# A two-layer graph-attention block on one Trainium2 core: centred linear weights, the context in four 64x64 tiles of the array, variance by squares on ScalarE, blocks prepared across passes, the first block in another order

## The chip, the cores and the metric

The kernel runs on one core of one Trainium2 chip. The core has a matrix engine (TensorE, PE in the profile; PEld is its weight load), a vector engine (VectorE, DVE), a scalar engine (ScalarE, ACT), GpSimd (POOL), and SyncE (SP), which here only issues DMAs. Each engine takes its own instructions in order and waits on semaphores for what others produce. The metric is the device time in microseconds (us) of one execution; the figure for a kernel is the median of its runs.

## The reference

The input `x` is 128 graphs of 64 nodes with 768 features, `adj` a 64x64 mask for each graph. All is fp32. First `h = max(layernorm(x), 0)`. Then two layers, each with three 768x768 weights:

```
u_left  = h @ (h @ W_left.T).T / sqrt(768)         # per graph, 64x64
u_right = h @ (h @ W_right.T).T / sqrt(768)
u       = u_left where j >= i, u_right where j < i, both masked by adj
e       = exp(u) * adj
att     = e / (sum(e, axis=2) + 1e-10)
ctx     = att @ (h @ W_lin.T + b_lin)
h       = max((ctx - mean(ctx)) / (std(ctx, ddof=1) + 0.001) * a + b, 0)
```

The result is `x + h`.

## The kernel before, in words

8192 tokens are cut into 16 *blocks* `u` of 512 tokens, and a block into four quarters `q` of 128 tokens (two graphs). A layer `l` is two *passes* over all blocks; what passes between them goes through DRAM (`H0`, `H1`: the activations, transposed; `ATT`: the attention, as a 128x128 block-diagonal tile for each quarter).

**Pass one** computes the scores. In layer 0 it also normalises `x` (`prepare`: `bn_stats` and `bn_aggr` at L156-157, square root L207, `norm` L194, `turn` with TensorE transposes L200 and ScalarE evictions L201). `project(u, k, g)` computes a third (`g`) of the left (`k=0`) or right (`k=1`) projection. A product of 2x2 blocks is done with seven block products instead of eight (Strassen-Winograd): the table `ORDER` has seven *groups* X, Y, Z, V, X, Z, V, each three matmuls into the PSUM bank of that name (L229), and each is evicted by DVE or ACT (L240 to L250). The seven need sums of the weights (`S1` to `S4`, `sums_w`, L96 to L100) and of the token blocks (`T1` to `T4`, tile `ts`, `sums_t`, L120 to L123, on POOL). `scores(u)` multiplies the block's tokens with the projections, 48 matmuls with 64 output columns each (L263; the two graphs of a quarter go to PSUM partitions 0-63 and 64-127), then mask, exp and division on DVE and ACT, four transposes (L293), and a store of the attention.

**Pass two** computes `h_lin` and the context. A block has two *rounds* `r`, one for each call of `linear(u, r)`: seven groups of three matmuls of 384 columns (L447), evicted by DVE (L452 to L468) with one helper addition on POOL (`u2b`, L457). After the first group of a round stands `finish` of the round before: `context` (L366) multiplies the 128x128 attention of a quarter with its `h_lin`, in two halves of 384 columns, for two quarters, four matmuls; then mean and variance by `bn_stats` on DVE (L156, L157, L380), square root on ACT (L383), reciprocal and bias on DVE (L385 to L388), and `z = ctx * rs + nb` on ACT (L391). In layer 0, `z` is transposed (L413) and evicted with scale, bias and relu (L416). In layer 1, POOL multiplies by `a` (L394) and adds `b` (L395), and DVE does relu and residual into `xr` (L397), which SP stores.

**What sets the order.** The program is written in the order in which each engine is to take its work; nothing reorders it. Small steps are put as functions in one deque (`queue`), and `pump(n)` between the groups emits the next `n`; `flush` emits all. In pass one, `pump(1)` follows each group; in pass two, `pump(3)`. At a pass's start `load(0)` and `prepare(0)` come ahead of the first group, and the sums for the next layer's weights are one step of that queue (`weights`), emitted between groups of blocks 1 and 2 of pass two. PSUM has eight banks: four for X, Y, Z, V (`ps_st`) and four for all else (`ps_aux`).

## Time and profile before

| | |
|---|---|
| three runs | 3298.9, 3294.8, 3292.9 us; median 3294.8 |
| the profiled execution | 3297.7 us, of which the span of the trace is 3295.9 |
| busy | PE 3095.9 us (94%), DVE 1269.5 (39%), POOL 867.5 (26%), ACT 557.6 (17%) |
| granted PE clock | 0.985 of full on average |
| pass one of layer 0 | first matmul group at 43.1 us; last scores end at 1050.8 |
| pass two of layer 0 | first context at 1084.1, last but one at 1649.6 |
| pass one of layer 1 | first group at 1686.4; last scores end at 2660.9 |
| pass two of layer 1 | first context at 2697.4, last but one at 3262.0 |

Reading notes. Each fp32 matmul of the program stands in the trace as two records (a group of three is "x6"). A busy share of PE says that something was in the array, not that it ran at its peak. In brackets behind a row stands how long its engine was idle just before and what ended that.

### The profile page before, as it was taken

Reading aid. Unit: us, or ns where it says so; the run is one execution under the profiler, and the core shown is the slowest. Engines: PE = TensorE matmul, PEld = TensorE weight load, DVE = VectorE, ACT = ScalarE, POOL = GpSimd, SP = SyncE. Lnnn points to the kernel's source line nnn. Section 1 sums busy time; section 2 is a strip of 40 time slices with the busy share of each in tenths; the row PEclk is TensorE's granted clock in tenths of the full one; section 3 lists DMA queues with packets and bytes.
Section 4 is the critical chain, followed back from the end, with each engine's and each line's share of the span. In section 5 each row is a group of like instructions: output and inputs, shape, how many; then the busy total and the mean of one; then the engine's idle time right before and its main releaser. Section 6 shows DMA issues by size and latency. Waiting matters only on the chain.

```text
span 3295.9 us, 37473 instructions
## 1 busy us (share of the span) xinstructions
PE 3095.9 (94%) x15232; PEld 2396.5 (73%) x15232; DVE 1269.5 (39%) x2906; ACT 557.6 (17%) x1169; POOL 867.5 (26%) x541
## 2 busy tenths in 40 slices
PE   5999999999998889999979999999999979898897
PEld 4888888888887555555568888888888855455454
DVE  4333334334332334444422222222222236666665
ACT  1112112111210223233311000000000001111111
POOL 3111111211210332232222211211111036667665
PEclk9999999999999999999989999999999989999999
DMA  4111211211201132322211101101001023343333
GB/s 167 67 52 46 84 48 49 83 46 52 73 37 56 70 112 86 122 83 83 102 64 55 52 26 36 42 26 49 29 26 52 4 91 122 129 150 126 134 128 108
DMA packets 77484, 244.64 MB, mean 74 GB/s; under 512 B 7936, under 2 KB 34048, under 8 KB 67072
## 3 DMA queue, kind: packets, MB, share of 16 engines
q1 hardware_dynamic: 77312, 242.25, 20.2%
q8 instruction: 120, 1.97, 0.2%
q14 instruction: 52, 0.43, 0.0%
HBM read 158.34 MB, written 83.89 MB: 73 GB/s over the span
## 4 chain that ended last, share of the span: by engine, by line
PE 81%; POOL 9%; DVE 5%; DMA 2%; ACT 1%; issue 1%; SPq 1%; POOLq 0%; ACTq 0%; DVEq 0%
PE Z L229 15%; PE V L229 15%; PE X L229 15%; PE Y L229 8%; PE X L447 6%; PE aux L263 5%; PE aux L366 5%; POOL z L395 4%; PE Y L447 4%; PE V L447 4%; POOL z L394 3%; PE Z L447 2%; DVE xr L397 2%; PE aux L413 1%; PE aux L200 1%; DVE u L455 1%
## 5 line engine op out<-in xcount | busy, mean ns | idle before, releaser
L120 POOL TENSOR_TENSOR ts<-ht 128x768 f32<-128x768 f32 x64 | 116.3, 1816 | 1505.5 <-ACT ht L201 742.9
L447 PE MATMUL X<-w_n_A,ht 128*128 128x384 f32 x768 | 282.2, 505 | 61.0 <-DVE n L464 36.4
L229 PE MATMUL X<-ht,w_l_A 128*128 128x256 f32 x1152 | 281.4, 380 | 12.8 <-DMA ht<-h 12.8
L447 PE MATMUL V<-w_n_A,ts 128*128 128x384 f32 x768 | 271.5, 490 | 22.7 <-DVE n L462 22.7
L229 PE MATMUL X<-ht,w_r_A 128*128 128x256 f32 x1152 | 280.0, 379 | 0.0
L229 PE MATMUL V<-ts,w_r_A 128*128 128x256 f32 x1152 | 280.0, 379 | 0.0
L229 PE MATMUL V<-ts,w_l_A 128*128 128x256 f32 x1152 | 280.0, 379 | 0.0
L250 DVE TENSOR_TENSOR n<-V,u 128x256 f32<-128x256 f32 x384 | 162.2, 422 | 284.5 <-PE V L229 283.5
L447 PEld LDWEIGHTS X<-w_n_A,ht 128*128 128x128 f32 x768 | 145.2, 196 | 169.2 <-DVE n L464 54.9
L243 DVE TENSOR_TENSOR u<-Y,s 128x256 f32<-128x256 f32 x192 | 81.5, 424 | 456.0 <-PE Y L229 452.9
L229 PEld LDWEIGHTS X<-ht,w_l_A 128*128 128x128 f32 x1152 | 219.4, 191 | 42.9 <-DMA ht<-h 13.1
L229 PEld LDWEIGHTS V<-ts,w_r_A 128*128 128x128 f32 x1152 | 217.8, 190 | 29.0
L229 PEld LDWEIGHTS X<-ht,w_r_A 128*128 128x128 f32 x1152 | 217.7, 190 | 29.0
L229 PEld LDWEIGHTS V<-ts,w_l_A 128*128 128x128 f32 x1152 | 217.7, 190 | 29.0
L447 PEld LDWEIGHTS V<-w_n_A,ts 128*128 128x128 f32 x768 | 141.1, 190 | 126.9 <-DVE n L462 20.9
L250 DVE TENSOR_TENSOR n<-Z,u 128x256 f32<-128x256 f32 x192 | 80.7, 421 | 359.1 <-PE Z L229 359.1
L457 POOL TENSOR_TENSOR u2b<-u,b 128x384 f32<-128x384 f32 x64 | 63.9, 998 | 574.9 <-DVE rs L385 574.9
L248 ACT COPY n<-X 128x256 f32<-128x256 f32 x192 | 71.5, 372 | 772.2 <-PE X L229 772.2
L397 DVE SCALAR_TENSOR_TENSOR xr<-z,xr 128x768 f32<-128x768 f32 x64 | 135.8, 2123 | 130.2 <-POOL z L395 130.2
L366 PE MATMUL aux<-n,at 128*128 128x384 f32 x512 | 176.1, 486 | 0.7 <-DVE n L464 0.5
L240 ACT COPY s<-X 128x256 f32<-128x256 f32 x192 | 71.6, 373 | 618.1 <-PE X L229 618.1
L263 PE MATMUL aux<-n,ht 128*64 128x128 f32 x3072 | 174.7, 274 | 0.0
(98 smaller groups left out, 4604.1 us busy)
## 6 DMA issues: line engine op xcount, KB each, us to landing
ht<-h SPq DMA_DIRECT2D x48, 1536.0 KB, 7.2
x<-in_x_dram SPq DMA_DIRECT2D x64, 384.0 KB, 7.2
h<-ht SPq DMA_DIRECT2D x16, 1536.0 KB, 6.2
h<-n SPq DMA_DIRECT2D x16, 1536.0 KB, 6.1
xr<-in_x_dram SPq DMA_DIRECT2D x64, 384.0 KB, 3.7
out_dram<-xr SPq DMA_DIRECT2D x64, 384.0 KB, 2.4
adj<-in_adj_dram SPq DMA_DIRECT2D x32, 256.0 KB, 3.5
att<-at SPq DMA_DIRECT2D x32, 256.0 KB, 2.0
```

The lines of the kernel that those rows point to most:

```text
L120: queue.append(lambda: nc.gpsimd.tensor_sub(b["T1"], b["B12"], b["B11"]))
L229: nc.tensor.matmul(p, w[a][:, c, g * P:(g + 1) * P], b[t][:, c, :], start=(new and c == 0), stop=(c == CH - 1), skip_group_check=True)
L240: nc.scalar.copy(s1, p)
L243: nc.vector.tensor_add(u2, p, s1)
L248: nc.scalar.copy(to, pb)
L250: nc.vector.tensor_add(to, pb, (u4 if i == 3 else u2).rearrange("p (b s) -> p b s", s=S))
L263: nc.tensor.matmul(p[h * S:(h + 1) * S, q, :], ht[:, c, b * S:(b + 1) * S], m[c // CH][:, c % CH, b].rearrange("p k j -> p (k j)"), start= ...
L366: nc.tensor.matmul(p[:, :HH], AT[u][:, q, :], hl[:, q, n * HH:(n + 1) * HH], start=True, stop=True)
L394: nc.gpsimd.tensor_mul(z, z, rows["a"])
L395: nc.gpsimd.tensor_add(z, z, rows["b"])
L397: nc.vector.scalar_tensor_tensor(xr, z, 0.0, xr, op0=ALU.max, op1=ALU.add)
L447: nc.tensor.matmul(p, b[t][:, c, r * P:(r + 1) * P], w[a][:, c, :], start=(new and c == 0), stop=(c == CH - 1), skip_group_check=True)
```

## The change

It has five parts.

1. *Centred weights.* `centre` subtracts from each row of `W_lin` its mean over the 768 outputs, and from `b_lin` its mean, so that `ctx` has mean zero. The steps are four DVE reductions of 128x1152 elements and four POOL subtractions for each layer, in the queue of pass one, block 1. Layer 0's `W_lin` is now loaded there too and not at the start.
2. *Variance by squares.* With mean zero, the variance is a sum of squares: one ACT instruction for a quarter (`AF.Square` with `accum_out`), one square root for both quarters, one add and one reciprocal on DVE. `bn_stats`, `bn_aggr`, the scaling of the variance and the bias `nb` are gone from pass two. In layer 1, DVE multiplies by `rs` and `a` in one instruction out of PSUM (`scaled`), POOL only adds `b`.
3. *Context in 64x64 tiles.* The attention is block-diagonal, so its two 64x64 blocks are multiplied apart: eight matmuls with 64 rows and 64 columns of weights, in four places of the array, into four different halves of two two-bank PSUM tiles. For quarters 2 and 3 the two graphs change places; layer 1 loads its adjacency in that order (three DMAs in place of one) and swaps back.
4. *Blocks prepared across passes.* The last block of a pass loads the next pass's first block and makes its token sums; the last transposes of a pass one stand in the next pass (`flush(keep=1)`); in pass two the token sums and the weight sums are single steps, one behind each group (`beside`).
5. *The first block.* The loads of `W_right` follow the first block, the normalisation goes quarter by quarter, and DVE makes the first sums.

`ps_aux` now has two tiles of two banks in place of four of one. The diff, with unchanged lines and repeated patterns left out:

```diff
-    ps_aux = ctx.enter_context(tc.tile_pool(name="ps_aux", bufs=4, space=bass.MemoryType.PSUM))
+    ps_aux = ctx.enter_context(tc.tile_pool(name="ps_aux", bufs=2, space=bass.MemoryType.PSUM))
...
-    def flush():
-        pump(len(queue))
+    def flush(keep=0):
+        pump(len(queue) - keep)
...
+    def centre(l):
+
+        t = W[l, "n"]
+        for a, b in (("A11", "A21"), ("A12", "A22")):
+            m = stat.tile([P, 2, CH], F32, name="wm", bufs=2)
+
+            def means(a=a, b=b, m=m):
+                nc.vector.reduce_sum(m[:, 0], t[a], axis=mybir.AxisListType.X)
+                nc.vector.reduce_sum(m[:, 1], t[b], axis=mybir.AxisListType.X)
+                nc.vector.tensor_add(m[:, 0], m[:, 0], m[:, 1])
+                nc.vector.tensor_scalar_mul(m[:, 0], m[:, 0], 1.0 / H)
+
+            queue.append(means)
+            for s in (a, b):
+                queue.append(lambda s=s, m=m: nc.gpsimd.tensor_sub(
+                    t[s], t[s], m[:, 0].unsqueeze(2).to_broadcast([P, CH, HH])))
...
         t = W[l, kind]
-        eng.tensor_add(t["S1"], t["A21"], t["A22"])
-        eng.tensor_sub(t["S2"], t["S1"], t["A11"])
...
-            def prepare(u):
+            def prepare(u, eng=nc.gpsimd):
...
-                    def turn(c):
-                        p = ps_aux.tile([P, T], F32, name="aux")
-                        for q in range(Q):
...
+                        nc.scalar.activation(ht[:, c0:c0 + 2, :], p, AF.Relu)
...
-                    for c in range(C):
+                        if u == 0:
+                            queue.append(lambda q=q: scale(q, q + 1))
+                            queue.append(lambda q=q: norm(q))
+                    if u:
+                        queue.append(lambda: scale(0, Q))
+                        for q in range(Q):
+                            queue.append(lambda q=q: norm(q))
+                    for c in range(0, C, 2):
                         queue.append(lambda c=c: turn(c))
                     queue.append(lambda: nc.sync.dma_start(H0[u], ht))
-                sums_t(key)
+                if key not in TS:
+                    sums_t(key, eng)
                 queue.append(lambda: masks(u))
...
-                p = ps_aux.tile([P, Q, 2 * S], F32, name="aux")
+                p = ps_aux.tile([P, 2, T], F32, name="aux")[:, 0].rearrange("p (q m) -> p q m", q=Q)
...
-                    if first:
-                        first()
-                    prepare(0)
+                    if l == 0:
+                        load_w(0, "l")
+                        prepare(0, nc.vector)
+
+                        flush(keep=5)
+                        tokens = [queue.popleft() for _ in range(5)]
+                        sums_w(0, "l", nc.vector)
+                        sums = [queue.popleft() for _ in range(4)]
+                        queue.extend(sums[:2] + tokens[:2] + [sums[2], tokens[2], sums[3], tokens[3], tokens[4]])
+                        load_w(0, "r")
+                        sums_w(0, "r", nc.gpsimd)
+                    else:
+                        prepare(0)
                     flush()
...
+                        else:
+                            load_h(2, l, 0)
+                            sums_t((2, l, 0))
                         if u in aside:
                             aside[u]()
...
-            flush()
+            flush(keep=1)
...
+            bm = stat.tile([P, 2], F32, name="bm", bufs=1)
+            nc.vector.reduce_sum(bm[:, 0:1], rows["b1"], axis=mybir.AxisListType.X)
+            nc.vector.reduce_sum(bm[:, 1:2], rows["b2"], axis=mybir.AxisListType.X)
+            nc.vector.tensor_add(bm[:, 0:1], bm[:, 0:1], bm[:, 1:2])
+            nc.vector.tensor_scalar_mul(bm[:, 0:1], bm[:, 0:1], -1.0 / H)
             nc.gpsimd.tensor_sub(rows["b2"], rows["b2"], rows["b1"])
+            nc.vector.tensor_scalar_add(rows["b1"], rows["b1"], bm[:, 0:1])
...
+            def context(u, r):
+
+
+                hl, at = HL[u], AT[u]
+                lo, hi = slice(0, S), slice(S, P)
+                cx = [ps_aux.tile([P, 2, T], F32, name="aux") for _ in range(2)]
                 for n in range(2):
-                    p = ps_aux.tile([P, T], F32, name="aux")
-                    nc.tensor.matmul(p[:, :HH], AT[u][:, q, :], hl[:, q, n * HH:(n + 1) * HH],
-                                     start=True, stop=True)
-                    cx.append(p[:, :HH])
-                z = sp.tile([P, H], F32, name="z", bufs=2 if last else 4)
-                Z[u, q] = z
+                    for (j, k, i) in ((lo, 0, lo), (hi, 0, hi), (lo, 1, hi), (hi, 1, lo)):
+                        q = r + 2 * k
+                        m = n if j == lo else 1 - n
+                        nc.tensor.matmul(cx[k][i, m, :HH], at[j, q, j], hl[j, q, m * HH:(m + 1) * HH],
+                                         start=True, stop=True)
+                return [c[:, :, :HH] for c in cx]
...
-                    xr = sp.tile([P, H], F32, name="xr", bufs=2)
-                    nc.sync.dma_start(xr, x_t[u][q])
-
-                def chain():
-                    mv = stat.tile([P, 2], F32, name="mv1")
-                    mean_var(mv, cx)
-
-                    var = stat.tile([P, 1], F32, name="var")
...
+                for k in range(2):
+                    nc.scalar.activation(zs[k].rearrange(two, n=2), cx[k], AF.Square, accum_out=ss[:, k:k + 1])
+
+                nc.scalar.activation(sd, ss, AF.Sqrt, bias=floor, scale=1.0 / (H - 1.0))
+                nc.vector.tensor_scalar_add(rs, sd, EPS_LN)
+                nc.vector.reciprocal(rs, rs)
+                if last:
+                    def scaled(k):
+                        nc.vector.scalar_tensor_tensor(
+                            zs[k].rearrange(two, n=2), cx[k], rs[:, k:k + 1],
+                            rows["a"].rearrange(two, n=2), op0=ALU.mult, op1=ALU.mult)
+                        nc.gpsimd.tensor_add(zs[k], zs[k], rows["b"])
+
+                    def done(k):
+                        nc.vector.scalar_tensor_tensor(xs[k], zs[k], 0.0, xs[k], op0=ALU.max, op1=ALU.add)
+                        nc.sync.dma_start(out_t[u][r + 2 * k], xs[k])
+
+                    queue.append(lambda: scaled(0))
+                    queue.append(lambda: scaled(1))
+                    queue.append(lambda: None)
+                    queue.append(lambda: done(0))
+                    queue.append(lambda: done(1))
...
+                def scaled():
+                    for k in range(2):
+                        nc.scalar.activation(zs[k].rearrange(two, n=2), cx[k], AF.Copy, scale=rs[:, k:k + 1])
...
+                queue.append(scaled)
+                queue.append(lambda: None)
                 for c0 in range(0, C, 2):
-                    queue.append(lambda c0=c0: part(c0))
+                    queue.append(lambda c0=c0: turn(c0))
                 if r == 1:
                     queue.append(lambda: nc.sync.dma_start(H1[u], OUT[u]))
 
...
-                    pump(3)
-
+                    elif i:
+                        pump(1)
+                    if aside:
+                        aside.popleft()()
+
+            load(0)
...
-                    linear(u, r, before)
+                    beside = deque()
                     if r == 0:
                         if u + 1 < NB:
                             load(u + 1)
+                        elif not last:
+                            load_h(1, 1, 0)
                         if u in aside:
-                            aside[u]()
-                    elif u + 1 < NB:
-                        prepare(u + 1)
-                        flush()
+                            loaded = aside[u]()
+                    else:
+                        kept = list(queue)
+                        queue.clear()
+                        if u + 1 < NB:
+                            sums_t((2, l, u + 1))
+                        elif not last:
+                            sums_t((1, 1, 0))
+                        if u in aside:
+                            loaded()
+                        beside.extend(queue)
+                        queue.clear()
+                        queue.extend(kept)
+                    linear(u, r, before, beside)
+                    while beside:
+                        beside.popleft()()
             finish(NB - 1, 1)
...
+    def one_aside(l):
+        def begin():
+            load_w(l, "n")
+            centre(l)
+            sums_w(l, "n", nc.gpsimd)
+        return begin
+
+    def two_aside(kind):
+        def begin():
+            load_w(1, kind)
+            return lambda: sums_w(1, kind, nc.gpsimd)
+        return begin
+
+    pass_one(0, {1: one_aside(0)})
+    pass_two(0, {1: two_aside("l"), 2: two_aside("r")})
+    pass_one(1, {1: one_aside(1)})
```

Three places show how the instructions now stand. In TensorE's stream, the border from pass one to pass two of layer 0, up to the third group of the new pass (`aux<-n,ht` are the scores of the last block, `aux<-ident,bd` the transposes of its attention). Before:

```order
L229 MATMUL Z<-ht,w_r_S_192 128x256 x3
L229 MATMUL V<-ts,w_r_A_188 128x256 x3
L263 MATMUL aux<-n,ht 64x128 x48
L293 MATMUL aux<-ident,bd_156 128x128 x4
L447 MATMUL X<-w_n_A_201,ht 128x384 x3
L447 MATMUL Y<-w_n_S_206,ts 128x384 x3
```

Now:

```order
L259 MATMUL V<-ts,w_r_A_250 128x256 x3
L293 MATMUL aux<-n,ht 64x128 x48
L497 MATMUL X<-w_n_A_674,ht 128x384 x3
L497 MATMUL Y<-w_n_S_679,ts 128x384 x3
L323 MATMUL aux<-ident,bd_158 128x128 x4
L497 MATMUL Z<-w_n_S_678,ts 128x384 x3
```

The transposes, which wait for the whole chain of DVE and ACT behind the scores, moved behind two groups of the next pass.

In TensorE's stream, one round of pass two, layer 0 (`aux<-n,at` is the context, `aux<-ident,z` the transposes of `z`). Before:

```order
L447 MATMUL X<-w_n_A_201,ht 128x384 x3
L366 MATMUL aux<-n,at 128x384 x4
L447 MATMUL Y<-w_n_S_206,ts 128x384 x3
L447 MATMUL Z<-w_n_S_205,ts 128x384 x3
L413 MATMUL aux<-ident,z 128x128 x4
L447 MATMUL V<-w_n_A_202,ts 128x384 x3
L413 MATMUL aux<-ident,z 128x128 x8
```

Now:

```order
L497 MATMUL X<-w_n_A_674,ht 128x384 x3
L417 MATMUL aux<-n,at 64x384 x8
L497 MATMUL Y<-w_n_S_679,ts 128x384 x3
L497 MATMUL Z<-w_n_S_678,ts 128x384 x3
L497 MATMUL V<-w_n_A_675,ts 128x384 x3
L470 MATMUL aux<-ident,z 128x128 x4
L497 MATMUL X<-w_n_A_677,ht 128x384 x3
L470 MATMUL aux<-ident,z 128x128 x4
```

The context is eight matmuls of 64 columns, and the transposes moved from behind the third group to behind the fourth, fifth and sixth, four each.

In DVE's stream, one round of pass two, layer 1 (`s`, `u`, `n` are evictions of the linear groups; `xr` is the residual step). Before, from the square root's return on:

```order
L455 TENSOR_TENSOR u_16937<-Y,s_16896 128x384
L385 TENSOR_SCALAR rs_16943<-sd_16941 128x1
L386 RECIPROCAL rs_16943<-rs_16943 128x1
L388 SCALAR_TENSOR_TENSOR nb_16946<-mv_16919,rs_16943 128x1
L460 TENSOR_TENSOR u_16956<-Z,u2b 128x384
L397 SCALAR_TENSOR_TENSOR xr<-z,xr 128x768
L462 TENSOR_TENSOR n<-V,u_16956 128x384
L397 SCALAR_TENSOR_TENSOR xr<-z,xr 128x768
L464 TENSOR_TENSOR n<-X,b_14144 128x384
L466 TENSOR_TENSOR n<-Z,u_16937 128x384
L468 TENSOR_TENSOR n<-V,u2b 128x384
```

Now:

```order
L438 TENSOR_SCALAR rs_15575<-sd_15574 128x2
L439 RECIPROCAL rs_15575<-rs_15575 128x2
L505 TENSOR_TENSOR u_15585<-Y,s_15555 128x384
L442 SCALAR_TENSOR_TENSOR z<-aux,rs_15575,a 128x768
L510 TENSOR_TENSOR u_15595<-Z,u2b 128x384
L442 SCALAR_TENSOR_TENSOR z<-aux,rs_15575,a 128x768
L512 TENSOR_TENSOR n<-V,u_15595 128x384
L514 TENSOR_TENSOR n<-X,b_13481 128x384
L448 SCALAR_TENSOR_TENSOR xr<-z,xr 128x768
L516 TENSOR_TENSOR n<-Z,u_15585 128x384
L448 SCALAR_TENSOR_TENSOR xr<-z,xr 128x768
L518 TENSOR_TENSOR n<-V,u2b 128x384
```

The two residual steps stood around the eviction of the first V group and now stand behind the second X and the second Z; both reads of `cx` for `z` are on DVE.

130 lines of the change are left out of this document (49 added, 81 removed).

## The prediction

> **What bounds the kernel now.** First the page: the shares by engine and the chain that ended last.
>
> ```profile
> PE 3095.9 (94%) x15232; PEld 2396.5 (73%) x15232; DVE 1269.5 (39%) x2906; ACT 557.6 (17%) x1169; POOL 867.5 (26%) x541
> PE   5999999999998889999979999999999979898897
> PE 81%; POOL 9%; DVE 5%; DMA 2%; ACT 1%; issue 1%; SPq 1%; POOLq 0%; ACTq 0%; DVEq 0%
> ```
>
> TensorE is the chain for 81%, and the slices below 9 say where it isn't: the start, pass two of layer 0 (slices 13 to 15), the borders of passes, and pass two of layer 1 (33 to 40). Both passes one are matmul back to back, and the change takes none from them. So I read the chain of waits in order of time, pass two of layer 0 (columns: start, us, what).
>
> ```profile
> 1084.06 2.58 PE aux L366 x8
> 1086.63 1.95 PE Y L447 x6
> ...
> 1093.56 0.87 PE aux L413 x8
> 1094.44 1.94 PE X L447 x6
> ...
> 1102.18 2.58 PE aux L366 x8
> ...
> 1649.59 2.58 PE aux L366 x8
> ```
>
> A round is 18.12 us (1084.06 to 1102.18): seven groups at 1.94, 13.58; the context, 2.58; twelve transposes at 0.87/8 = 0.11, 1.31. That is 17.47; the other 0.65 is TensorE waiting on `z`. From the first context to the last in the loop are 565.5 us, 30 rounds. 30 x 18.12 is 543.6; the other 22 us are two long stalls, which the timeline shows on TensorE and on POOL:
>
> ```profile
> 1129.69 2.62 POOL L96 TENSOR_TENSOR w_l_S<-w_l_A,w_l_A 128x1152 f32<-128x1152 f32 x1 [21.33 <-DMA w_l_A<-in_w_left_dram]
> 1141.72 3.58 PE L447 MATMUL Z<-w_n_S,ht 128*128 128x384 f32 x6 [9.81 <-DVE u L460]
> 1188.67 4.00 PE L447 MATMUL Z<-w_n_S,ht 128*128 128x384 f32 x6 [9.75 <-DVE u L460]
> ```
>
> The weight sums, as one step, stand in POOL's queue and wait for their DMA; behind them waits `u2b`, for it DVE, for that TensorE.
>
> Pass two of layer 1, the timeline of two rounds:
>
> ```profile
> 2902.26 3.90 PE L447 MATMUL X<-w_n_A,ht 128*128 128x384 f32 x6 [2.03 <-DVE n L464]
> ...
> 2920.28 0.96 DVE L397 SCALAR_TENSOR_TENSOR xr<-z,xr 128x768 f32<-128x768 f32 x1 [1.23 <-POOL z L395]
> ...
> 2933.76 1.81 POOL L394 TENSOR_TENSOR z<-z,a 128x768 f32<-128x768 f32 x1
> 2933.83 2.54 DVE L397 SCALAR_TENSOR_TENSOR xr<-z,xr 128x768 f32<-128x768 f32 x1 [2.76 <-POOL z L395]
> 2935.64 2.40 POOL L395 TENSOR_TENSOR z<-z,b 128x768 f32<-128x768 f32 x1
> 2936.30 0.55 DVE L462 TENSOR_TENSOR n<-V,u 128x384 f32<-128x384 f32 x1
> 2936.90 2.20 PE L447 MATMUL V<-w_n_A,ts 128*128 128x384 f32 x6 [0.69 <-DVE n L462]
> ```
>
> DVE takes `xr` ahead of the eviction of V, and waits for POOL's multiply and add. While POOL runs, `xr` takes 2.54 instead of 0.96: it starts 0.07 after POOL's instruction and ends 0.8 after that one's end. So DVE is late, and TensorE with it; after 2.03 us of idleness its group even takes 3.90 instead of 2.10. In the chain:
>
> ```profile
> 2697.40 2.58 PE aux L366 x8
> ...
> 3262.00 2.58 PE aux L366 x8
> ```
>
> 564.6 us for 30 rounds, 18.82 each, of which TensorE needs 13.58 + 2.58 = 16.16.
>
> **The change part by part.** The *context* is the open price: the kernel has no matmul with 64 rows of weights. What it has is `scores`, with two 64-column places. The timeline cut off after 50, 200 and 300 ns, and at the end:
>
> ```profile
> 167.75 0.33 PE L263 MATMUL aux<-n,ht 128*64 128x128 f32 x2
> ...
> 167.75 0.44 PE L263 MATMUL aux<-n,ht 128*64 128x128 f32 x4
> ...
> 167.75 0.55 PE L263 MATMUL aux<-n,ht 128*64 128x128 f32 x6
> ```
>
> Records start in pairs, a pair each 0.11 us, which is what one record of 128 columns alone takes (a transpose, 0.11). So the two places work beside one another, at full rate, from the first pair on; 96 records take 5.39 us in the chain (its rows further down), 48 x 0.109 = 5.23 and 0.16 for the change of array shape. With as much for the way back I put 0.35 us. Four places at full rate: eight matmuls cost as two, 2 x 0.645 (a third of a group) = 1.29, plus 0.35, 1.64 us. Bounds: 1.64 if all four run together; 8 x 0.645 + 0.35 = 5.51 if none does. I take 1.64, since both places of the nearest row lose nothing; this is the largest risk.
>
> The Trainium skill (TensorE: Matmul & The Clock Gate, Part 3, Measured speedup) gives 3.07 for four row tiles, not 4: a context of 5.16/3.07 + 0.35 = 2.03, and 25 us more over 64 of them, an estimate. No row here has row tiles.
>
> *Layer 0, pass two.* A round is 13.58 + 1.31 + 1.64 = 16.53 if nothing else stalls. The transposes now come one to three groups later. Their input: two squares on ACT from 1.65 us after the context's start, 768 elements each; by
>
> ```profile
> L391 ACT ACTIVATE z<-aux,nb,rs 128x384 f32<-128x384 f32 x256 | 157.7, 667 | 69.4 <-DVE nb L388 69.1 <-DVE rs L385 0.3
> L201 ACT ACTIVATE ht<-aux 128x512 f32<-128x512 f32 x96 | 57.1, 597 | 80.4 <-PE aux L200 78.6
> L452 DVE TENSOR_TENSOR s<-X,b 128x384 f32<-128x384 f32 x64 | 35.7, 557 | 126.2 <-PE X L447 126.2
> L120 POOL TENSOR_TENSOR ts<-ht 128x768 f32<-128x768 f32 x64 | 116.3, 1816 | 1505.5 <-ACT ht L201 742.9 <-DMA ht<-h 711.3 <-PE V L229 51.3
> ```
>
> about 1.0 each (597 for 512 elements, in proportion, and some more for the sum); then root and reciprocal, 0.7, and two scalings: 6.4, while the fourth group ends at 7.5. Hidden, with 1 us to spare. The eviction of Y waits on DVE behind the reciprocal until 4.4; it is needed by the third group's eviction at 5.5. The weight sums, single steps half a block after their DMA, no longer hold `u2b`: POOL has 4 x 1.8 + 4 x 2.6 + 1.0 = 18.6 us in such a round, with `u2b` near its front. So 30 x 16.53 = 496 for 565.5: **69.6 less**.
>
> *Layer 1, pass two.* TensorE needs 13.58 + 1.64 = 15.22. DVE: seven evictions 3.9, two `scaled` out of PSUM (two of 557, near 1.0 each), two `xr` 0.96 to 2.54, 0.3 small: 8.1 to 11.3. POOL: two additions 3.6, `u2b` 1.0, in every second round 7.2 of token sums: 11.8 at most. Both fit. What is late next: with token sums, `xr` meets a busy POOL twice; counted through, the last V's eviction ends 15.2 us after the context's start, just as the next context wants it. I give 0.13 on average, 15.35: 30 x 15.35 = 460.5 for 564.6, **104.1 less**. The removed `bn_stats` themselves give nothing; DVE had room.
>
> *Borders and start.* Chain and timeline:
>
> ```profile
> 1045.33 5.42 PE aux L263 x96
> ...
> 1748.09 5.39 PE aux L263 x96
> 1808.51 5.39 PE aux L263 x96
> ...
> 2655.47 5.42 PE aux L263 x96
> ```
>
> ```profile
> 14.45 1.36 DVE L96 TENSOR_TENSOR w_l_S<-w_l_A,w_l_A 128x1152 f32<-128x1152 f32 x1 [12.07 <-DMA w_l_A<-in_w_left_dram]
> ...
> 25.97 1.01 DVE L156 BATCH_NORM_STATS2 st<-x 128x6 f32<-128x384 f32 x2
> ...
> 46.18 1.56 PE L229 MATMUL Y<-ts,w_l_S 128*128 128x256 f32 x6 [1.64 <-POOL ts L121]
> ...
> 1066.45 3.66 PE L447 MATMUL X<-w_n_A,ht 128*128 128x384 f32 x6 [11.09 <-issue]
> ...
> 1686.43 2.93 PE L229 MATMUL X<-ht,w_l_A 128*128 128x256 f32 x6 [12.82 <-DMA ht<-h]
> ...
> 2679.44 4.18 PE L447 MATMUL X<-w_n_A,ht 128*128 128x384 f32 x6 [13.48 <-DMA ht<-h]
> ...
> 3291.74 0.96 DVE L397 SCALAR_TENSOR_TENSOR xr<-z,xr 128x768 f32<-128x768 f32 x1 [1.69 <-POOL z L395]
> ```
>
> First border, scores to first context: 38.7 us. Without a gap 5.4, eight groups 15.5, transposes and shape 0.7: 21.6, so **17.1 less**. The third: 41.9; its bias rows land late, as their place is that of the last mask, and the first eviction waits, 1.6: 23.2, **18.7 less**. The second, from the last context in the loop to the first scores: 98.5. Now 14.6 for the rest of the round, 8.2 for the last context with its wait on ACT and twelve transposes, 3 for slow groups after that idleness (the 2.93 above is 1.29 at full speed), 57 for 44 groups of pass one (a block of 60.42 less scores and four transposes is 42 groups, 1.29 each): 82.8, **15.7 less**. Start: `x` lies ahead of `W_left` in the queue; by bytes, 1.5 of 4.1 MB before 14.45 us, it is there by 5.4. Then four quarters in series on DVE and ACT (1.0 + 0.2 + 0.5 + 0.2 + 0.75 each) with one table load, 12; transposes and evictions 5; one sum on DVE: Y at about 23 instead of 46.2, **23 less** (12 if `W_left`'s sums get in between, 27 at best). End: 33.9 from the last context in the loop; now 13.6 to the last context, 10.6 through squares, `scaled`, addition and two `xr`, 3.2 for the store: 27.4, **6.5 less**.
>
> Centring: 8 POOL and 8 DVE instructions in passes one, hidden by POOL idle there (1505.5 us before L120) and DVE idle. DVE's row for 768 elements of reduction is not there; twice 1.36 a step, under the 5 us that four PSUM banks give; without that cover 10 us in all.
>
> Sum: 69.6 + 104.1 + 17.1 + 18.7 + 15.7 + 23 + 6.5 = 254.7. Against the profiled execution: 3297.7 - 254.7 = 3043.0; it lies 2.9 above the median 3294.8, so **3040**.
>
> **The rivals.** (a) *Two places at a time, not four.* Then a context is 4 x 0.645 + 0.35 = 2.93, 64 x 1.29 = 83 more: 3123. For it: no row shows more than two. A rule of the Trainium skill (TensorE: Matmul & The Clock Gate, Part 3, What overlaps and what doesn't) goes this way: matmuls start and end in program order. As the two records of a matmul share a place, the second would hold back the next place: nine steps of 0.322 + 0.35, 3.25 us, 3143. By that rule the scores would begin with a lone record; the trace has two within the first 50 ns, so it speaks against it. (b) *POOL and DVE take over in layer 1.* If the meeting with token sums costs 2 us in every second round and, as at 2902.26, 1.8 more for the slow group behind it: 15 x 3.8 = 57, 3097. For it the 2.54; against it, that V's eviction is no longer behind the first `xr`. (c) *The context's eight matmuls run one by one*, 5.51: 3.87 x 64 = 248 more, 3288, hardly better than before. (d) The other side: *one by one, and each change of place empties the array*, 0.15 more for each: about 6.6, 64 x 4.96 = 317 more, 3357. From 5.6 us for a context the change is slower than before (254.7/64 + 1.64). Against it, the scores, which change place with each matmul. (e) *The change doesn't do what it says:* first blocks are not ready at the borders, since a DMA waits for a buffer; 51 us back, 3091.
>
> **How the numbers follow.** Forecast 0.64 (its own range 3020 to 3075), (a) 0.18, (b) 0.07, (e) 0.04, (c) 0.04, (d) 0.03. The range 3020 to 3142 holds the first, (b), (e) and most of (a). About 0.2%, 6.6 us, is what a measurement of this kernel tells from no change: slower is (d), 0.03; within it, half of (c) and a little, 0.03; faster, 0.94.
>
> **What would show it.** Right: contexts near 1.6 us in the chain, rounds of 16.5 and 15.3, no idleness of TensorE over 5 us between 25 us and the end, a first Y near 23. Wrong: eight context matmuls over 2.9 us; an idle time before X or the context in layer 1 put down to `n`; idleness at a border put down to a DMA.

## The result, and the profile after

The changed kernel takes 3040.95 us (median; 3040.0 to 3042.56), the one before 3295.96 on the same chip (3292.92 to 3298.92). The ratio is 0.9227, with a 95% interval of 0.9211 to 0.9243: 255 us less, and 3040 us had been predicted. The profiled execution took 3040.96 us, its span is 3039.2, and its granted clock was 0.998 (0.985 before).

The page of the changed kernel, with the rows that answer to those shown of before:

```profile
PE 3001.1 (99%) x15744; PEld 2328.2 (77%) x15744; DVE 1061.3 (35%) x2231; ACT 551.6 (18%) x1124; POOL 765.5 (25%) x486
PE   7999999999999999999999999999999999999998
PE 97%; DVE 1%; DMA 1%; ACT 0%; issue 0%; POOL 0%; DVEq 0%; POOLq 0%; ACTq 0%; SPq 0%
```

TensorE is now 97% of the chain (81% before), and of the slices only the first and the last are not full. About half of what is left beside it, some 40 of 81 us of the chain, lies at the two ends.

The chain of waits of the changed kernel (start, us, what), in order of time: pass two of layer 0, then of layer 1, and the scores (line 293) at the three borders. The context is line 417:

```profile
1023.55 5.39 PE aux L293 x96
...
1045.20 1.45 PE aux L417 x16
1046.65 2.13 PE Y L497 x6
1048.78 1.94 PE Z L497 x6
...
1061.71 1.45 PE aux L417 x16
...
1540.52 1.45 PE aux L417 x16
...
1623.27 5.39 PE aux L293 x96
...
2532.19 5.42 PE aux L293 x96
...
2829.18 1.45 PE aux L417 x16
...
2844.37 1.45 PE aux L417 x16
...
3011.50 1.45 PE aux L417 x16
```

A context is 1.45 us, and the Y group behind it 2.13 instead of 1.94: 1.64 in all, the predicted price, with the 0.35 for the change of shape split into 0.16 ahead (1.45 less 2 x 0.645) and 0.19 behind. (The chain puts its cuts at ends. By the starts of first records, 0.10 of it already stands ahead of the context: the last X group takes 2.03 us instead of 1.93, the context 1.45, and Y 2.04.) Rounds of layer 0 are 16.51 us and rounds of layer 1 15.19, without a gap of TensorE, but for one of 15.97 that is told of below. How the span divides, each stage from one first record of a context or of scores to the next:

| stage | before, us | after, us | less | predicted |
|---|---|---|---|---|
| start, to the first scores | 104.7 | 82.3 | 22.4 | 23 |
| pass one, layer 0 | 940.6 | 941.2 | -0.6 | 0 |
| first border | 38.6 | 21.7 | 17.0 | 17.1 |
| pass two, layer 0 (30 rounds) | 565.5 | 495.3 | 70.2 | 69.6 |
| second border | 98.6 | 82.8 | 15.9 | 15.7 |
| pass one, layer 1 | 907.4 | 908.9 | -1.5 | 0 |
| third border | 41.8 | 22.7 | 19.1 | 18.7 |
| pass two, layer 1 (30 rounds) | 564.6 | 456.6 | 108.0 | 104.1 |
| end | 34.1 | 27.8 | 6.3 | 6.5 |

The sum of the column "less" is 256.8, the spans differ by 256.7.

How the four places work together is seen when the timeline of TensorE in the changed kernel is cut off shortly after a context's start: after 45, 405 and 1485 ns (the matmul records so far are the last number of a row):

```profile
1177.21 0.55 PE L417 MATMUL aux<-n,at 64*64 64x384 f32 x4
...
1177.21 0.88 PE L417 MATMUL aux<-n,at 64*64 64x384 f32 x8
...
1177.21 1.52 PE L417 MATMUL aux<-n,at 64*64 64x384 f32 x16
```

Each of the eight matmuls leaves two records. Four records start at once, 20 ns from the first to the last; the next four start 0.37 us after the first, and the others in steps of 0.32: all four places run together from the start, and the sixteen records are done in four steps.

In layer 1, DVE in a round with token sums in the changed kernel, and one row of POOL:

```profile
2808.22 0.56 DVE L514 TENSOR_TENSOR n<-X,b 128x384 f32<-128x384 f32 x1 [1.38 <-PE X L497]
2808.69 2.02 DVE L448 SCALAR_TENSOR_TENSOR xr<-z,xr 128x768 f32<-128x768 f32 x1
2810.64 0.55 DVE L516 TENSOR_TENSOR n<-Z,u 128x384 f32<-128x384 f32 x1
2811.11 2.09 DVE L448 SCALAR_TENSOR_TENSOR xr<-z,xr 128x768 f32<-128x768 f32 x1
2813.12 0.55 DVE L518 TENSOR_TENSOR n<-V,u2b 128x384 f32<-128x384 f32 x1
```

```profile
2809.85 2.53 POOL L135 TENSOR_TENSOR ts<-ht 128x768 f32<-128x768 f32 x1
```

Both `xr` still meet a busy POOL (2.02 and 2.09 instead of 0.96, and POOL's own sum 2.53 instead of 1.81), but neither row of `xr` shows a wait for `z`, and the last V is evicted by 2813.67. The next context starts at 2813.92. In the other rounds with token sums the first `xr` mostly takes 1.73, and the last V is evicted 0.54 us ahead of the next context; without token sums it is 1.27.

Once the eviction does come too late, in the first round of the pass. There a table load on ACT stands ahead of the square root, everything behind it is 1.3 us later, and the second `xr` waits for POOL. The next context starts on time but has to wait for the last half of `n`: it takes 2.23 instead of 1.45, and the round is the one of 15.97.

```profile
2558.11 1.28 ACT L437 ACT_TABLE_LOAD   x1
...
2567.76 2.55 DVE L448 SCALAR_TENSOR_TENSOR xr<-z,xr 128x768 f32<-128x768 f32 x1 [0.92 <-POOL z L445]
```

```profile
2570.11 2.23 PE aux L417 x16
```

### The profile page after: what moved, and what is told of

Read it like the earlier page. It is cut to its first block, busy times and chain, and to the rows that moved or that the text cites. A ratio compares the mean times of both kernels' runs of the same rounds, so it can differ in the third digit from the quotient of the medians.

```text
span 3039.2 us, 37771 instructions
## 1 busy us (share of the span) xinstructions
PE 3001.1 (99%) x15744; PEld 2328.2 (77%) x15744; DVE 1061.3 (35%) x2231; ACT 551.6 (18%) x1124; POOL 765.5 (25%) x486
## 3 DMA queue, kind: packets, MB, share of 16 engines
q8 instruction: 124, 2.03, 0.3%
## 4 chain that ended last, share of the span: by engine, by line
PE 97%; DVE 1%; DMA 1%; ACT 0%; issue 0%; POOL 0%; DVEq 0%; POOLq 0%; ACTq 0%; SPq 0%
PE Z L259 16%; PE V L259 16%; PE X L259 16%; PE Y L259 8%; PE Z L497 8%; PE V L497 8%; PE X L497 8%; PE aux L293 6%; PE Y L497 4%; PE aux L417 3%; PE aux L470 1%; PE aux L226 1%; PE aux L323 0%; DMA x<-in_x_dram 0%; DVE bd L317 0%
## 5 line engine op out<-in xcount | busy, mean ns | idle before, releaser
L135 POOL TENSOR_TENSOR ts<-ht 128x768 f32<-128x768 f32 x126 | 238.7, 1894 | 1541.3 <-ACT ht L228 742.7
L497 PE MATMUL X<-w_n_A,ht 128*128 128x384 f32 x768 | 269.0, 486 | 0.3 <-DVE s L502 0.3
L135 POOL TENSOR_TENSOR ts<-ht,ts 128x768 f32<-128x768 f32 x126 | 239.3, 1899 | 7.7 <-ACT ht L228 6.4
L435 ACT ACTIVATE z<-aux 128x768 f32<-128x768 f32 x128 | 102.6, 807 | 566.5 <-PE aux L417 566.5
L293 PEld LDWEIGHTS aux<-n,ht 128*64 128x64 f32 x3072 | 167.0, 137 | 10.6 <-issue 10.6
```

The source lines that it names most:

```text
L135: queue.append(lambda o=o, m=m, n=n: eng.tensor_sub(b[o], b[m], b[n]))
L293: nc.tensor.matmul(p[h * S:(h + 1) * S, q, :], ht[:, c, b * S:(b + 1) * S], m[c // CH][:, c % CH, b].rearrange("p k j -> p (k j)"), start= ...
L435: nc.scalar.activation(zs[k].rearrange(two, n=2), cx[k], AF.Square, accum_out=ss[:, k:k + 1])
L497: nc.tensor.matmul(p, b[t][:, c, r * P:(r + 1) * P], w[a][:, c, :], start=(new and c == 0), stop=(c == CH - 1), skip_group_check=True)
```

## Experiments

Times are medians, beside the changed kernel's 3041; ratios are to the kernel before on the same chip. The runs were taken in four sets, in which the kernel before took 3296.0 to 3298.5, so differences of up to 3 us between sets tell nothing. "Rounds" are the distances of first context records in the profiled execution.

**The context as full matmuls, all else as changed.**

```diff
-                for n in range(2):
-                    for (j, k, i) in ((lo, 0, lo), (hi, 0, hi), (lo, 1, hi), (hi, 1, lo)):
+                for k in range(2):
+                    for n in range(2):
                         q = r + 2 * k
-                        m = n if j == lo else 1 - n
-                        nc.tensor.matmul(cx[k][i, m, :HH], at[j, q, j], hl[j, q, m * HH:(m + 1) * HH],
+                        nc.tensor.matmul(cx[k][:, n, :HH], at[:, q, :], hl[:, q, n * HH:(n + 1) * HH],
...
-                if l == 0:
-                    nc.sync.dma_start(adj, adj_t[u])
-                else:
-                    nc.sync.dma_start(adj[:, :2], adj_t[u][:, :2])
-                    nc.sync.dma_start(adj[:S, 2:], adj_t[u][S:, 2:])
-                    nc.sync.dma_start(adj[S:, 2:], adj_t[u][:S, 2:])
+                nc.sync.dma_start(adj, adj_t[u])
```

> The changed kernel with its context as four full 128x128 matmuls again (the zero halves of the weights multiplied too), and the adjacency loaded in one piece in layer 1, since no halves are exchanged any more. Everything else stays. Theory (the context is on the path of TensorE in both layers, and the four places save what the chain shows, 2.58 less 1.65): rounds of 16.51 + 0.93 = 17.44 in layer 0 and 15.19 + 0.93 = 16.12 in layer 1, 64 x 0.93 = 60 us more, 3100. Rival (the gain of the rounds came from the variance, the weight sums and the order of the last steps; TensorE would only wait where it now multiplies): less than 20 us more, under 3061.

Measured: 3097.5 us, ratio 0.9396 (0.9382 to 0.9410), 56.5 us more. Rounds 17.44 and 16.12, both as the theory had them. The chain of that kernel (its context is line 410):

```profile
1046.05 2.58 PE aux L410 x8
1048.63 1.94 PE Y L490 x6
...
1063.49 2.58 PE aux L410 x8
```

2.58 for the context and a plain 1.94 for Y, against 1.45 and 2.13: in the changed kernel the saving of the four places arrives whole.

**The 64x64 context alone, in the kernel before.**

```diff
+            def contexts(u, r):
...
+                cx = [[ps_aux.tile([P, T], F32, name="aux")[:, :HH] for _ in range(2)] for _ in range(2)]
                 for n in range(2):
-                    p = ps_aux.tile([P, T], F32, name="aux")
-                    nc.tensor.matmul(p[:, :HH], AT[u][:, q, :], hl[:, q, n * HH:(n + 1) * HH],
+                    for (j, k, i) in ((lo, 0, lo), (hi, 0, hi), (lo, 1, hi), (hi, 1, lo)):
+                        q = r + 2 * k
+                        m = n if j == lo else 1 - n
+                        nc.tensor.matmul(cx[k][m][i], at[j, q, j], hl[j, q, m * HH:(m + 1) * HH],
                                      start=True, stop=True)
...
-                a = context(u, r)
+                cx = contexts(u, r)
+                a = context(u, r, cx[0])
                 pump(1)
-                b = context(u, 2 + r)
+                b = context(u, 2 + r, cx[1])
```

(And the adjacency of layer 1 in three pieces, as in the change.)

> The kernel before with only the 64x64 context (all eight matmuls at once, in four PSUM tiles of one bank, with the halves exchanged and undone in layer 1 as in the change); variance by bn_stats, order of the steps, POOL's multiply, weight sums and borders as before. Theory (alone it is off the path: in layer 0 the transposes wait for z, whose chain on DVE begins 0.36 us later for the first tile and goes through both in series; in layer 1 DVE's wait for POOL sets the round): rounds of 18.1 and 18.8 as before, TensorE waiting longer for z or n instead, 3296 +- 12. Rival (the 0.93 us fall straight through): 64 x 0.93 = 60 less, 3236; or in layer 0 alone, 29 less, 3267.

Measured: 3306.4 us, ratio 1.0031 (1.0021 to 1.0041): 9 us slower than the kernel before. The contexts are as short as in the changed kernel (1.46 in the chain), but rounds went from 18.06 and 18.19, in turn, to 18.24 and 18.33 in layer 0, and from 17.80 and 19.38 to 17.92 and 19.51 in layer 1. The waits of TensorE (line, what it waited for, us in total, times, longest), first in the kernel before, then with the 64x64 context alone:

```profile
PE V L447 <- DVE n L462: 22.7, 31, 0.8
PE aux L413 <- ACT z L391: 16.5, 31, 2.3
```

```profile
PE V L460 <- DVE n L475: 55.3, 31, 1.8
PE aux L425 <- ACT z L403: 42.7, 33, 3.9
```

These two rows have 58.8 us more, and the contexts save 64 x 0.93 = 59.5: what TensorE no longer multiplied, it waited. Of the spans' difference (3302.6 less 3295.9, 6.7) layer 0 has 7.9, 4.5 in its regular rounds and 3.4 in the two with the stalls, while layer 1 is 1.4 shorter: its regular rounds are longer too, but one round of 21 us stands there instead of four. Why the regular rounds are longer: between the first record of a context and the group that waits for `z` or `n`, the time is set by the steps of DVE and ACT, so what is saved there is waited. The part of the change of array shape that stands ahead of that record adds to the round. By first records, the last X group ahead of a context takes 2.03 us in layer 0 instead of 1.93 (in layer 1 2.13 instead of 2.04). It takes 2.03 in the changed kernel too, and 1.93 again in the run with full matmuls. In this stretch TensorE waits for nothing that could hide it. Behind the context little is later: DVE's `bn_stats` no longer begins while the second tile's context is still running, which makes the first tile's steps 0.52 later, but the last small DVE step before `z`, that of the second tile, starts 5.57 us after the context's first record before, and 5.60 with all eight matmuls first:

```profile
1214.44 2.74 PE L366 MATMUL aux<-n,at 128*128 128x384 f32 x8
...
1220.01 0.86 DVE L388 SCALAR_TENSOR_TENSOR nb<-mv,rs 128x1 f32<-128x1 f32 x1
```

```profile
1218.02 1.52 PE L376 MATMUL aux<-n,at 64*64 64x384 f32 x16
...
1223.62 0.86 DVE L400 SCALAR_TENSOR_TENSOR nb<-mv,rs 128x1 f32<-128x1 f32 x1
```

So of the 0.12 to 0.18 us by which regular rounds are longer, 0.09 to 0.10 stand ahead of the context, and 0.03 (layer 1) to 0.07 (layer 0, on average) between the context and the V that waits. The same edit is worth 56 us behind the other edits and costs 9 without them.

**The same eight matmuls, written place after place.**

```diff
-                for n in range(2):
-                    for (j, k, i) in ((lo, 0, lo), (hi, 0, hi), (lo, 1, hi), (hi, 1, lo)):
+                for (j, k, i) in ((lo, 0, lo), (hi, 0, hi), (lo, 1, hi), (hi, 1, lo)):
+                    for n in range(2):
```

> The changed kernel with the eight context matmuls written place after place: both halves of the first 64x64 place, then both of the second, and so on. The same matmuls, the same places. Theory (each place takes its own matmuls as they come, and one that waits for its place does not hold back the next place): contexts of 1.65 us, 3041. Rival A (strictly in the order of the program: each waits for the one ahead to start): with two records of 0.322 for a matmul, place after place, 12 steps of 0.322 before the last place starts its last record, 4.2 + 0.35 us a context, 64 x 2.9 = 185 us more, 3226. Rival B (a place may run ahead, but only a few records deep; in the changed kernel three records wait at most when the fourth place starts, here nine would): in between, with two places together and then two, 2.58 + 0.35 = 2.93, 64 x 1.28 = 82 more, 3123.

Measured: 3042.0 us, ratio 0.9226 (0.9210 to 0.9241): no difference that can be measured. The timeline of TensorE in that kernel, cut off 20 and 60 ns after a context's start:

```profile
1178.28 0.55 PE L417 MATMUL aux<-n,at 64*64 64x384 f32 x2
...
1178.28 0.57 PE L417 MATMUL aux<-n,at 64*64 64x384 f32 x4
```

Four places again start together, now 13 ns apart instead of 6.5: four records of a place pass for each start, where it was two. (A row doesn't name its place; but on one place records follow one another in steps of 0.32 us.) The rounds are 16.53 and 15.21, longer by the 0.02 us that the fourth place now starts later. Three records of each earlier place wait while the next place starts. So a place takes its own matmuls as they come, and those that wait for it do not hold back the others, at least nine records deep. Both rivals are out.

By the rule of the Trainium skill (TensorE: Matmul & The Clock Gate, Part 3, What overlaps and what doesn't), that matmuls start strictly in the order of the program, this kernel would have gone to about 3226 us. Here the first matmul of the fourth place, the seventh in the program, starts 40 ns after the first; the second matmul of the first place has its own first one ahead of it, two records of 0.322.

**Two places on one PSUM bank.**

```diff
-                        m = n if j == lo else 1 - n
+                        m = n
```

> The changed kernel without the exchange of halves between the upper and the lower place: both places that write to one PSUM tile now take the same half at the same time, so two places write to one bank (to different partitions of it) at once, where each of the four had a bank of its own. Theory (a place is a matter of the array alone): 1.65 us a context, 3041. Rival (a bank takes the results of one place at a time): the two places of a tile take turns, 4 x 0.645 + 0.35 = 2.93 us a context, 64 x 1.28 = 82 more, 3123.

Measured: 3038.6 us, ratio 0.9217 (0.9204 to 0.9231); rounds 16.51 and 15.19, and the same starts in fours. The exchange of halves is not needed for time: upper and lower place may write to different partitions of one bank at once. The 2.3 us below the changed kernel I don't count as a gain: no stage of the trace shows one that is in the context.

A rule of the Trainium skill (TensorEngine Tiling (Array Packing), Gotcha 1: PSUM Pressure) says that different row tiles can't use one bank at the same time. For two row tiles that write to different partitions no wait shows here.

**Variance by bn_stats again.**

```diff
-                    nc.scalar.activation(zs[k].rearrange(two, n=2), cx[k], AF.Square, accum_out=ss[:, k:k + 1])
+                    mean_var(mv[:, k], [cx[k][:, 0], cx[k][:, 1]])
...
-                nc.scalar.activation(sd, ss, AF.Sqrt, bias=floor, scale=1.0 / (H - 1.0))
+                nc.scalar.activation(sd, mv[:, :, 1], AF.Sqrt, bias=floor, scale=H / (H - 1.0))
```

> The changed kernel with its variance from bn_stats and bn_aggr on DVE (four instructions of 0.56 and two of 0.2 a round), where two squares and their sums on ACT stand now; the mean of bn_aggr is left unused, as the weights stay centred. Theory (DVE has room, so the removed bn_stats themselves give nothing): layer 0 unchanged, 16.51, since its transposes have about 1 us to spare and the chain gets 0.65 longer; layer 1 at most a few tenths more in rounds with token sums: 3041 to 3047. Rival (in layer 1 the last V's eviction just fits, so the 2.7 us of DVE come out whole in every second round): 15 x 2.7 = 40 more, 3081.

Measured: 3044.1 us, ratio 0.9226 (0.9212 to 0.9240): no difference that can be measured. Layer 0 keeps its 16.51, but for two rounds of 16.7. In layer 1 the chain of that kernel shows, in rounds that follow token sums, a context of 1.72 instead of 1.45, where it begins before the last half of `n` is there:

```profile
2833.82 1.45 PE aux L417 x16
...
2849.02 1.72 PE aux L417 x16
```

That is 0.28 in every second round, some 4 us, of the 2.4 us that DVE does more in each. The rest goes into idle time of DVE. The step "the removed bn_stats themselves give nothing" holds, to those 4 us.

**The multiply by ln_a back on POOL.**

```diff
-                        nc.vector.scalar_tensor_tensor(
-                            zs[k].rearrange(two, n=2), cx[k], rs[:, k:k + 1],
-                            rows["a"].rearrange(two, n=2), op0=ALU.mult, op1=ALU.mult)
+                        nc.vector.tensor_scalar(zs[k].rearrange(two, n=2), cx[k], rs[:, k:k + 1], None,
+                                                op0=ALU.mult)
+                        nc.gpsimd.tensor_mul(zs[k], zs[k], rows["a"])
```

> The changed kernel with the multiply by ln_a in layer 1 back on POOL (two instructions of 1.8 a round, between the scaling and the addition of b), DVE only scaling. The order of the steps stays, so xr is still taken behind the eviction of X. Theory (POOL's part of the chain is what layer 1 waited for): POOL has 3.65 + 3.65 + 1.0 + 8.7 = 17.0 us in a round with token sums, over the 15.19 of TensorE, and xr finds its input late and POOL busy: 2 to 4 us in every second round, 15 x 3 = 45 more, 3086. Rival (POOL has room over two rounds, 25.3 of 30.4 us, and the gain came from the later xr alone): within 8 us, 3041 to 3049.

Measured: 3120.3 us, ratio 0.9457 (0.9443 to 0.9471), 79 us more, not 45. Rounds are, in turn, 16.3 to 16.5 and 18.4 to 20.0 (once 21.4); the longer ones begin with a context that waits for the last V of a round with token sums. I had expected the shorter kind to stay at 15.19. DVE's timeline in that kernel, a round without token sums ahead of `xr` and one with them:

```profile
2693.99 2.55 DVE L448 SCALAR_TENSOR_TENSOR xr<-z,xr 128x768 f32<-128x768 f32 x1 [1.24 <-POOL z L445]
2696.46 0.55 DVE L518 TENSOR_TENSOR n<-V,u2b 128x384 f32<-128x384 f32 x1
...
2712.37 2.54 DVE L448 SCALAR_TENSOR_TENSOR xr<-z,xr 128x768 f32<-128x768 f32 x1 [3.12 <-POOL z L445]
2714.84 0.55 DVE L518 TENSOR_TENSOR n<-V,u2b 128x384 f32<-128x384 f32 x1
```

In both the second `xr` waits for POOL (1.24 and 3.12) and then takes 2.5, as a POOL instruction starts beside it; V's last eviction is behind it, and the context waits for that. What counts is not POOL's sum of work over two rounds but when its second addition ends. This is the largest single cause in layer 1: 75 of its 108 us come back with this one edit.

**Both xr one group earlier.**

```diff
                     queue.append(lambda: scaled(1))
-                    queue.append(lambda: None)
                     queue.append(lambda: done(0))
```

> The changed kernel with both xr of layer 1 one group earlier, the first directly behind V's first eviction. Theory (by the timeline POOL's first addition is done about 8 to 10 us after the context's start and the second about 11.5; with ln_a on DVE the place of xr no longer decides, since the last V's eviction still ends about 15.1): 3038 to 3046. Rival (the later place of xr is what keeps DVE from waiting for POOL): 1 to 2 us in each round with token sums, 15 x 1.5 = 22 more, 3063.

Measured: 3040.0 us, ratio 0.9215 (0.9200 to 0.9230): no difference. With token sums DVE does wait for POOL, but ends in time:

```profile
2810.05 2.55 DVE L448 SCALAR_TENSOR_TENSOR xr<-z,xr 128x768 f32<-128x768 f32 x1 [1.23 <-POOL z L445]
...
2812.99 0.54 DVE L517 TENSOR_TENSOR n<-V,u2b 128x384 f32<-128x384 f32 x1
```

So once POOL has one instruction less for each tile, this one step in the place of `xr` decides nothing. Its old place, around V's first eviction, was not tried.

**The weight sums in pass two of layer 0: as one lump, and as one lump behind a late load.**

```diff
             load_w(1, kind)
-            return lambda: sums_w(1, kind, nc.gpsimd)
+            sums_w(1, kind, nc.gpsimd)
+            four = [queue.pop() for _ in range(4)][::-1]
+            queue.append(lambda: [f() for f in four])
+            return lambda: None
```

> The changed kernel with the sums of W_left and W_right of layer 1 (in pass two of layer 0) as one step right behind their load, as the kernel before had them, not as four steps half a block later. Theory (POOL waits for the load, then has four sums of 2.6; u2b behind them is late, and with it DVE and TensorE): two stalls of 7 to 11 us, 14 to 22 more, 3055 to 3063. Rival (a round of 16.5 us without bn_stats hides it): within 4 us, 3041 to 3045.

Measured: 3042.1 us, ratio 0.9219 (0.9204 to 0.9235). The theory fell: no round of layer 0 is longer than 16.51. The first sum in POOL's timeline:

```profile
1069.63 2.63 POOL L115 TENSOR_TENSOR w_l_S<-w_l_A,w_l_A 128x1152 f32<-128x1152 f32 x1 [1.92 <-DMA w_l_A<-in_w_left_dram]
```

It waits 1.9 us for its load, where it was 21.3 before: in the changed kernel the load is asked for ahead of the block's first round, before it was asked for behind it. The sums also stand behind this round's `u2b` here (it started at 1066.71), where they stood ahead of it before. The next run undid both:

```diff
-            load_w(1, kind)
-            return lambda: sums_w(1, kind, nc.gpsimd)
+            def later():
+                load_w(1, kind)
+                sums_w(1, kind, nc.gpsimd)
+                four = [queue.pop() for _ in range(4)][::-1]
+                queue.appendleft(lambda: [f() for f in four])
+            return later
```

> The changed kernel with the loads of W_left and W_right of layer 1 asked for only in the second round of their block, and their sums as one step in that round, ahead of its u2b. In the run with the lump alone the loads were asked for a round earlier, and POOL waited 1.9 us for them. Theory (what stalled the kernel before was not the lump but POOL waiting for the load, 21.3 us, ahead of a u2b): two waits of POOL of 12 to 22 us and two stalls of TensorE of 7 to 13 us, 15 to 26 more than the changed kernel, 3056 to 3067. Rival (bn_stats on DVE, which are gone, made the stall): within 4 us, 3041 to 3045.

Measured: 3066.6 us, ratio 0.9301 (0.9287 to 0.9315), 25.7 more; two rounds of 29.80 and 28.22, the others 16.51. POOL's timeline and TensorE's waits in that kernel:

```profile
1088.79 2.61 POOL L115 TENSOR_TENSOR w_l_S<-w_l_A,w_l_A 128x1152 f32<-128x1152 f32 x1 [20.29 <-DMA w_l_A<-in_w_left_dram]
```

```profile
PE Z L497 <- DVE u L510: 21.1, 3, 11.0
```

These are the two stalls of the kernel before. Two things meet in them: POOL waits for the load, and then the four sums, 10.4 us, still stand ahead of `u2b`. The first such `u2b` starts at 1099.18, and the one before it at 1067.50. In the changed kernel these two are 16.6 us apart (1066.21 and 1082.79), so this one is 15 us late. Four sums in one step are harmless when their load is there and `u2b` is ahead of them. A late load with single steps was not tried.

**Without the preparation across passes.**

```diff
                             prepare(u + 1)
-                        else:
-                            load_h(2, l, 0)
-                            sums_t((2, l, 0))
...
-            flush(keep=1)
+            flush()
...
             load(0)
+            sums_t((2, l, 0))
+            flush()
             for u in range(NB):
...
-                        elif not last:
-                            load_h(1, 1, 0)
...
-                        elif not last:
-                            sums_t((1, 1, 0))
```

> The changed kernel without the preparation across passes: the first block of a later pass is loaded and its token sums are taken when the pass begins, as in the kernel before. Theory (the three borders each lose the time of a load and its first sums, during which TensorE has nothing): 17 + 16 + 17 = 50 more, 3091, with idle times of 11 to 13 us before X that the trace puts down to the load of ht or to no releaser at all. Rival (loads at the border overlap with the last scores and evictions anyway, since the other steps have become faster): 25 or less, under 3066.

Measured: 3093.1 us, ratio 0.9374 (0.9360 to 0.9388), 52 more. The borders are 39.8, 98.2 and 41.7 us again (after: 21.7, 82.8 and 22.7), and TensorE's waits show the loads:

```profile
PE X L494 <- DMA ht<-h: 24.7, 2, 13.5
...
PE X L259 <- DMA ht<-h: 12.3, 1, 12.3
```

**The old order of the first block.**

```diff
-                        prepare(0, nc.vector)
-
-                        flush(keep=5)
-                        tokens = [queue.popleft() for _ in range(5)]
                         sums_w(0, "l", nc.vector)
-                        sums = [queue.popleft() for _ in range(4)]
-                        queue.extend(sums[:2] + tokens[:2] + [sums[2], tokens[2], sums[3], tokens[3], tokens[4]])
                         load_w(0, "r")
-                        sums_w(0, "r", nc.gpsimd)
+                        sums_w(0, "r", nc.vector)
+                        flush()
+                        prepare(0)
```

> The changed kernel with the old order of the first block: the sums of W_left and W_right first, on DVE, then the block's normalisation, and its token sums on POOL. Theory (DVE waits for both weights before it takes x, which has been there since about 5 us): first Y at 44 to 47 instead of 21.5, 23 to 25 more, 3064 to 3066. Rival (the start is bound by the transfers, x of the next block and W_right included): 12 or less, under 3053.

Measured: 3061.1 us, ratio 0.9282 (0.9268 to 0.9296), 20 more. TensorE's first transpose and first Y in that kernel, then the first Y of the changed kernel and a group of the first block that still waits there, and last the row of DVE in the changed kernel that this group waited for:

```profile
28.59 0.45 PE L226 MATMUL aux<-ident,x 128*128 128x128 f32 x1 [28.59 <-DVE x L219]
...
43.66 1.56 PE L259 MATMUL Y<-ts,w_l_S 128*128 128x256 f32 x6 [1.89 <-POOL ts L135]
```

```profile
21.54 1.56 PE L259 MATMUL Y<-ts,w_l_S 128*128 128x256 f32 x6 [1.00 <-DVE ts L135]
...
37.87 1.56 PE L259 MATMUL Z<-ht,w_l_S 128*128 128x256 f32 x6 [1.82 <-DVE u L276]
```

```profile
33.76 1.02 DVE L170 BATCH_NORM_STATS2 st<-x 128x6 f32<-128x384 f32 x2 [3.72 <-DMA x<-in_x_dram]
```

Y is 22.1 us later, just under the theory's 23, but the first scores only 19.9: in the changed kernel the start is so early that the second block's `x` is late, and DVE, held by it, lets TensorE wait 1.8 us.

**A version with four small waits taken away.** Left in the changed kernel's trace are, among TensorE's waits:

```profile
PE aux L470 <- ACT z L463: 3.9, 2, 3.4
PE aux L323 <- DVE bd L317: 3.4, 5, 0.7
```

```diff
+                            queue.append(lambda q=q: nc.scalar.activation(
+                                sd[:, q:q + 1], mv[:, q:q + 1, 1], AF.Sqrt, bias=eps_in))
+                            for o in ([q - 1] if q else []) + ([q] if q == Q - 1 else []):
+                                queue.append(lambda q=o: nc.vector.reciprocal(rs[:, q:q + 1], sd[:, q:q + 1]))
+                                queue.append(lambda q=o: norm(q))
...
                     yield
                     yield
+                    yield
                     pt = ps_aux.tile([P, 2, T], F32, name="aux")[:, 0].rearrange("p (q m) -> p q m", q=Q)
...
+                        if k and u == NB - 1 and r:
+                            nc.vector.tensor_scalar(zs[k].rearrange(two, n=2), cx[k], rs[:, k:k + 1], None,
+                                                    op0=ALU.mult)
...
+            BIAS[l] = {}
+            for name, n0 in (("b1", 0), ("b2", HH)):
+                t = BIAS[l][name] = const.tile([P, HH], F32, name=name)
```

(The loads of the two bias rows stand with those of W_lin, in pass one.)

> The changed kernel with four small waits of its trace taken away: one more step between the softmax and the attention transposes (TensorE waits 3.4 us for bd in all); in the last round of layer 0 one of the two scalings on DVE beside ACT's (TensorE waits 3.9 for z, of which about 1 is to be had); the bias rows of pass two loaded during pass one (1.6 at the third border); in the first block the statistics of a quarter taken on DVE while ACT takes the root of the quarter ahead (3 x 0.45). Theory: 3.4 + 1 + 1.6 + 1.4 = 7 less, 3034. Rival (each is hidden by the next wait in line): within 2 us of 3041.

Measured: 3031.6 us (3031.07 to 3032.41), ratio 0.9192 (0.9178 to 0.9206), 9.4 us or 0.3% below the changed kernel, whose own times begin at 3040.0; 7 had been expected. By stages of the trace: first scores 2.0 earlier, the second border 1.5 shorter, the blocks of pass one of layer 1 all at 60.42 (several of the changed kernel's are 61.3), 5.2 less in all, the third border 1.1 shorter; 9.8 of span. The four edits were not tried one by one, and the second border is 81.4 to 82.8 us in runs in which nothing was done to it (81.3 here), so its 1.5 is not shown to come from the edit.

## Why the prediction was right

*What bounds the kernel.* That TensorE's own work, waits on `z` and `n`, two stalls and the borders make up the time was right, and each part that was undone alone brought its piece back: the context 56.5, ln_a on POOL 79, borders 52, the place of the weight load 25.7, the start 20. These are 233 of 255 us; the waits on `z` in layer 0, 0.65 in each of 30 rounds, and the end were not undone alone.

*Context.* 1.64 predicted, 1.64 measured. The two column places of `scores`, at full rate from their first pair, were the right row to go by: four places with rows and columns lose nothing either. Rivals (a), (c) and (d) are out by the rows in fours, as is the estimate of 2.03, and the place-after-place run shows that the order of writing doesn't matter. That the price falls through to the time only because the waits behind it are gone too is what the run with the context alone adds; the prediction had it in its sums (16.16 of need in rounds of 18.82) and did not say it.

*Layer 0.* 16.51 for 16.53. The 0.65 of waiting on `z` went as counted, and not through the squares: with `bn_stats` rounds are 16.51 too. By what is left it went through the later place of the transposes; that was not tried apart. For the two stalls the step gave two reasons, "single steps half a block after their DMA". Neither is needed: one lump right behind its load costs nothing, as long as the load is asked for a round earlier and the lump stands behind `u2b`. The late load with the lump ahead of `u2b` costs 25.7. That the load is now asked for ahead of the block's first round, the step did not name. What the late load and the place of the lump are worth each alone stays open.

*Layer 1.* 108.0 less instead of 104.1: the 0.13 a round for the meeting of `xr` with POOL, 3.9 us in all, was put too high. The place of the edge was right. In rounds with token sums the last V's eviction ends about 0.54 us before the next context (0.25 in the rows shown), and where the square root was 1.3 us late the meeting did cost 0.78, but in one round only. With `bn_stats`, 2.4 us more of DVE cost 0.28 in every second round. So rival (b) did not come about, with about half a microsecond to spare. What decides is when POOL's second addition ends: moved back by the multiply, it costs 75 us in this pass.

*Borders, end.* All within 0.5 us. At the second border this is partly luck: the last context with its wait and the transposes took 9.6 us (1555.10 to 1564.68 in the chain) and not 8.2, and the slow groups behind it 1.6 and not 3; and the stage itself is 81.4 to 82.8 in runs that left it alone. The late bias rows were there as foreseen at the third border; loading them earlier took 1.1 of the predicted 1.6 away.

*Start.* Y came at 21.54 instead of 23, and yet only 22.4 of the predicted 23 are left by the first scores: the second block's `x`, which the prediction did not follow, is the next to be late.

*Centring* was put at nothing. The block in which it is queued takes 63.78 us instead of 63.05 in layer 0 and 61.15 instead of 60.42 in layer 1. In both, the chain goes through the four steps of the second `means` on DVE, 3.4 us ahead of an eviction that TensorE wants: 0.7 us for each layer. No run takes the centring out alone.

## What to carry to other kernels

Price a shorter matmul only together with what waits behind it: here the same edit was worth 56 us once the waits for DVE and POOL were gone, and cost 9 us alone, since TensorE waited for the same results as before and part of the change of array shape came on top. For an engine beside the critical one look not at its load but at the end of the one instruction that somebody waits for, and at what stands in the queue ahead of it; here a load that was asked for one round too late, with its work ahead of what TensorE needed, cost 26 us, and the same work with its load in time nothing. Block-diagonal operands can use four places of the array at once: here the row of the kernel's own two-place matmul was enough to predict it.
